# A planner's durations set anew: restarts, row groups, chained instructions and steps between engines

## The chip, the cores and the metric

The kernel runs on one core of one Trainium2 chip. The metric is the device time of one execution in microseconds (us), as a median over runs. One execution was also profiled, and all rows below come from that one.

## The reference, cut to what matters

A transformer layer works on x of 8 x 512 x 256 in f32. It is layer-normed; then an attention part and a feed-forward part are added to x.

```python
xn = _layernorm(x)
# attention, 16 heads of 16: three branches
k_c, v_c = blocks(k) @ Wck, blocks(v) @ Wcv        # 32 blocks of 16 tokens
out_c = softmax(mask(q @ k_c.T / 4)) @ v_c         # compressed
top_idx = top_k(logits_c, 4)                       # 4 blocks for each query
out_s = softmax(q @ k[top_idx].T / 4) @ v[top_idx] # selected
out_l = softmax(window(q @ k.T / 4, 32)) @ v       # local window
out = (g0 * out_c + g1 * out_s + g2 * out_l) @ Wo
# feed-forward: product-key experts and a gated layer
sc, ix = top_k(einsum(xn @ Wq, keys), 8)           # two halves, 4 heads
idx, scores = best 8 of the 8 x 8 sums             # of 1024 experts
w = silu(xn @ down_embed[idx]) * softmax(scores)
mlp = silu(xn @ Wg + bg) * (xn @ Wu + bu) @ Wd + bd
x = x + out + mlp + w @ up_embed[idx]
```

## The kernel before

The work is cut into 8 rows of 512 tokens (the batch), 32 tiles of 128 tokens (4 to a row) and 16 halves of 256 tokens. For each row, `layernorm`, `prepare_keys` and `prepare_values` make the transposed input xnT, keys, values and gates. For each tile, `queries` and `logits` compute the compressed logits and the maxima of the scores by block (bm) and by window (ml); `select` picks the four blocks and extends the queries (ext, qx) by the mask; `weights` makes score blocks of 128 x 128 for all 16 heads and takes their exponential into wT; `products` multiplies wT with the values; `compressed` and `finish` normalise (rzn), gate and turn the heads back to tokens through `by_token` (results atc and at). `choose_experts` finds the best keys with MAX8 and FIND_INDEX8 and turns them into tables; `route` spreads them over 1024 experts on VectorE (big) and GpSimd (gw); `experts` applies all 1024 experts densely (aT). For each half, `hidden` makes the gated layer (xg, hT) in eight slices, whose weights wb come by DMA one slice at a time, and multiplies with Wd; `project` multiplies aT with up_embed (ue_s) and the attention with Wo, and adds to yo.

Heads are 16 wide and lie in row groups of 32 partitions. The score and product matmuls therefore use only a quarter of the array, and four of them with different `tile_position` can run beside each other; the program marks such stretches with `con.share = 4`. In the trace an f32 matmul leaves two records, a transpose or a bf16 matmul one.

Each engine works through its own queue in the order in which the program wrote it[...]. The order is written by a planner, the class `Conductor`, while the program is built. Every stage above is a Python generator that goes over its items and is a job of its own. At a `yield` it names the engine that it needs next and the buffers or events that it needs first; what lies between two yields is a step, issued without interruption. `run` (line 237) asks `begin` (227) for each job's earliest start by the plan's clock. Of the jobs that can start no later than 0.12 us (`NEAR`, 172) after the first, the one with the lowest rank is taken (about the oldest tile), and `step` (220) lets it issue its instructions. Every instruction passes `book` (184), which adds an assumed duration to its engine's time `at` and so sets when engine, result and buffers are taken to be free. The assumptions are constants: a fixed part and a part by element for each engine (170, 171), a cost by column for matmuls, a divisor for row groups, an extra for a few slow operations, and `HOP` (169), the time from a result on one engine to its use on another. `book` also keeps VectorE's two-input instructions that read no PSUM and GpSimd's work apart, as the two are taken to share a port. A wrong duration breaks nothing, since semaphores hold whatever comes early: it makes an order in which an instruction stands in its queue ahead of what it waits for, and all behind it waits too.

PSUM is given out as two pairs of banks for scores and four single banks for all the rest (283, 284). After the set-up the planner's clocks are put to zero (436), then the jobs are added and run.

```python
    HOP = {"PE": 0.3, "DVE": 0.2, "ACT": 0.23, "POOL": 0.2, "SP": 2.5, None: 0.0}
    ...
            first = min(s for s, _ in ready)
            s, j = min((r for r in ready if r[0] <= first + self.NEAR), key=lambda r: r[1].rank)
```

Of the kernel before, what the change touches and what calls it, by code (L numbers as in the profile page):

```python
# [9 lines left out]
BF16 = mybir.dt.bfloat16  # L10
# [6 lines left out]
P = 128  # L17
# [89 lines left out]
class Event:  # L107


    def __init__(self):  # L110
        self.time = None
# [52 lines left out]
class Conductor:  # L164
# [1 line left out]

    HOP = {"PE": 0.3, "DVE": 0.2, "ACT": 0.23, "POOL": 0.2, "SP": 2.5, None: 0.0}
    FIXED = {"DVE": 0.07, "ACT": 0.07, "POOL": 0.26}  # L170
    EACH = {"DVE": 1.04e-3, "ACT": 0.83e-3, "POOL": 1.9e-3}
    NEAR = 0.12

    def __init__(self, psum):
        self.psum = psum
        self.at = dict.fromkeys(("PE", "DVE", "ACT", "POOL", "SP"), 0.0)
        self.busy = dict.fromkeys(self.at, 0.0)
        self.port = {"DVE": (0.0, 0.0), "POOL": (0.0, 0.0)}
        self.jobs, self.cur, self.share = [], Job(None, 0), 1

    def later(self):
        return self.cur.end + self.HOP[self.cur.eng]

    def book(self, eng, op, args, kw):
        aps = [a for a in [*args, *kw.values()] if hasattr(a, "shape")]
        n = max(int(np.prod(a.shape[1:])) for a in aps)
        if eng == "PE":
            if op == "transpose":
                cost = 0.11
            else:  # L190
                n = int(np.prod(args[2].shape[1:]))
                cost = (n * 0.42e-3 if args[2].dtype == BF16 else max(n, 32) * 1.68e-3) / self.share
        elif eng == "SP":
            cost = 0.06
        else:
            each = self.EACH[eng]
            if eng == "DVE" and all(a.dtype == BF16 for a in aps):
                each /= 2
            cost = self.FIXED[eng] + each * n
            if op in ("match_replace", "max_index", "tensor_tensor_reduce"):  # L200
                cost += 0.08
        j = self.cur
        start = max(self.at[eng], j.end + (self.HOP[j.eng] if eng != j.eng else 0.0))
        if eng == "POOL" or eng == "DVE" and op in ("tensor_tensor", "scalar_tensor_tensor") and not any(
                a.tensor is self.psum.tensor for a in aps):

            s, e = self.port["DVE" if eng == "POOL" else "POOL"]
            if s <= start:
                start = max(start, e)
            self.port[eng] = (start, start + cost)  # L210
        self.at[eng] = start + cost
        self.busy[eng] += cost
        j.end, j.eng = start + cost, eng
# [4 lines left out]
        self.step(j, None)  # L218

    def step(self, j, got):  # L220
        self.cur = j
        try:
            j.req = j.gen.send(got)
        except StopIteration:
            self.jobs.remove(j)

    def begin(self, j):
        eng, *res = j.req
        s = j.end + (self.HOP[j.eng] if eng is not None and eng != j.eng else 0.0)
        for r in set(res):  # L230
# [6 lines left out]
    def run(self):  # L237
        while self.jobs:
# [9 lines left out]
            else:  # L248
                j.end = max(j.end, s - self.HOP[j.eng])
            got = [r.take() for r in j.req[1:]]  # L250
# [1001 lines left out]
```

## Time and profile before

| what | value |
|---|---|
| median of 3 runs | 1812.65 us (1808.81 to 1814.56) |
| the profiled execution's own time | 1813.57 us |
| its span, first to last instruction | 1811.8 us |
| TensorE (PE) busy | 1622.0 us, 90% |
| VectorE (DVE) busy | 1478.4 us, 82% |
| GpSimd (POOL) busy | 1012.4 us, 56% |
| ScalarE (ACT) busy | 686.5 us, 38% |
| mean granted TensorE clock | 0.97 |
| DMA | 31 GB/s on average |
| chain of work that ended last | PE 55%, DVE 36%, ACT 3% |

PE is the matmul engine, and PEld its weight loads, which run beside it. Line numbers in the rows are all L160, since every instruction passes one helper; the tile names tell the groups apart. A row of the groups or of the timeline gives output<-input, shapes, count and duration; in brackets stands how long the engine was idle before and what released it. Durations of instructions that follow each other overlap in part on VectorE and TensorE, so the distance of two starts says more about what one occupies than its own duration. The first 60 us are set-up and loading.

### The profile page before, as it was taken

To read this page: it belongs to the slowest core of one execution; us is meant where nothing else is said; L and a number is where in the kernel's file an instruction comes from. 1 tells how busy PE (TensorE), PEld (TensorE's weight loads), DVE (VectorE), ACT (ScalarE), POOL (GpSimd) and SP (SyncE) were. 2 spreads that over 40 slices of the span, in tenths; PEclk is the share of its full clock that TensorE was granted. 3 is DMA by queue.
4 is the path that set the end of the run, shared out by engine and by line. 5 is a ranking of instruction groups with operands and counts; after the bars stand their busy time and mean duration, and the time that the engine had idled before them with its cause. 6 is when DMAs were issued, how large, how long until landed. Compare 5 with 4: busy or idle time off the path is not lost.

```text
span 1811.8 us, 47633 instructions
## 1 busy us (share of the span) xinstructions
PE 1622.0 (90%) x19208; PEld 1246.5 (69%) x19208; DVE 1478.4 (82%) x5292; ACT 686.5 (38%) x1370; POOL 1012.4 (56%) x789
## 2 busy tenths in 40 slices
PE   3889879899899998999989998989979999898969
PEld 2667757777677766767667676766757777676757
DVE  2598799886977889898898967788897897979892
ACT  1344323444335243352343533344324434433233
POOL 2066546646475365665476754656647456575644
PEclk9999989999999999999999998999989999998989
DMA  5001001111001100001011110101001010100001
GB/s 181 10 21 37 19 19 31 31 40 24 24 25 37 37 26 25 24 26 38 16 34 31 32 31 20 36 26 37 25 18 31 15 40 28 31 19 24 25 11 32
DMA packets 55069, 56.12 MB, mean 31 GB/s; under 512 B 21696, under 2 KB 38080, under 8 KB 54848
## 3 DMA queue, kind: packets, MB, share of 16 engines
q1 hardware_dynamic: 54848, 53.07, 9.8%
q8 instruction: 151, 2.47, 0.6%
q14 instruction: 70, 0.57, 0.1%
HBM read 48.02 MB, written 4.19 MB: 29 GB/s over the span
## 4 chain that ended last, share of the span: by engine, by line
PE 55%; DVE 36%; ACT 3%; issue 3%; POOL 1%; DMA 1%; SPq 0%; DVEq 0%; ACTq 0%; POOLq 0%
PE psum L160 55%; DVE bm L160 6%; DVE big L160 4%; DVE pick L160 3%; DVE ixu L160 2%; DVE ml L160 2%; DVE mr L160 2%; DVE aT L160 2%; ACT wT L160 2%; DVE junk L160 2%; DVE hT L160 1%; DVE sums L160 1%; DVE top L160 1%; DVE at_x L160 1%; DVE xg L160 1%
## 5 line engine op out<-in xcount | busy, mean ns | idle before, releaser
L160 POOL TENSOR_TENSOR big<-big,ed 128x1024 f32<-128x1024 f32 x224 | 486.1, 2170 | 411.9 <-DVE big L160 359.2
L160 ACT ACTIVATE wT<-psum 128x1024 f32<-128x1024 f32 x224 | 217.6, 1021 | 167.6 <-PE psum L160 167.6
L160 PE MATMUL psum<-xnT,wb 128*128 128x256 f32 x1024 | 255.2, 393 | 9.1 <-DVE hT L160 5.6
L160 POOL TENSOR_TENSOR gw<-gw,big 128x1024 f32<-128x1024 f32 x96 | 228.1, 2376 | 7.0
L160 DVE TENSOR_REDUCE bm<-psum 128x32 f32<-128x512 f32 (+2 forms) x224 | 199.1, 911 | 32.3 <-PE psum L160 32.1
L160 PEld LDWEIGHTS psum<-xnT,wb 128*128 128x128 f32 x1024 | 191.7, 196 | 46.7 <-DVE hT L160 8.2
L160 DVE SCALAR_TENSOR_TENSOR big<-rc 128x1024 f32<-128x1024 f32 x128 | 167.6, 1309 | 19.5 <-POOL gw L160 19.5
L160 PE MATMUL psum<-wT,v 128*32 128x128 f32 x3584 | 138.4, 279 | 25.7 <-ACT wT L160 24.9
L160 PE MATMUL psum<-qx,k 32*128 32x128 f32 (+1 forms) x4352 | 149.6, 271 | 11.0 <-DVE ml L160 9.1
L160 PEld LDWEIGHTS psum<-qx,k 32*128 32x128 f32 (+1 forms) x4352 | 123.8, 175 | 38.9 <-issue 17.8
L160 PEld LDWEIGHTS psum<-wT,v 128*32 128x32 f32 x3584 | 86.6, 109 | 78.7 <-ACT wT L160 50.6
L160 PE MATMUL psum<-xnT,deT_s 128*128 128x128 f32 x1024 | 131.9, 284 | 5.0 <-DVE aT L160 2.7
L160 PEld LDWEIGHTS psum<-xnT,deT_s 128*128 128x128 f32 x1024 | 126.0, 199 | 12.1 <-DVE aT L160 3.7
L160 PE MATMUL psum<-wd_s,hT 128*128 128x256 f32 x512 | 121.1, 382 | 0.0
L160 DVE SCALAR_TENSOR_TENSOR aT<-aT,psum 128x512 f32<-128x512 f32 x128 | 87.3, 682 | 38.9 <-ACT aT L160 31.4
L160 PE MATMUL psum<-k,q 32*128 32x384 f32 (+3 forms) x1024 | 113.9, 486 | 5.2 <-DVE ml L160 3.7
L160 PE MATMUL psum<-ue_s,aT 128*128 128x256 f32 x512 | 117.1, 381 | 0.0
L160 ACT ACTIVATE xg<-psum,bgh 128x256 f32<-128x256 f32 x128 | 60.7, 474 | 142.3 <-PE psum L160 140.1
L160 PEld LDWEIGHTS <-cbf 128*128 128x128 bf16 x856 | 69.1, 102 | 58.7 <-issue 30.6
L160 PEld LDWEIGHTS psum<-ue_s,aT 128*128 128x128 f32 x512 | 95.2, 190 | 15.5 <-issue 2.0
L160 PEld LDWEIGHTS psum<-wd_s,hT 128*128 128x128 f32 x512 | 94.1, 190 | 15.1 <-issue 2.6
L160 ACT COPY qx<-psum 128x512 f32<-128x512 f32 x80 | 47.0, 587 | 140.1 <-PE psum L160 126.9
(161 smaller groups left out, 3170.5 us busy)
## 6 DMA issues: line engine op xcount, KB each, us to landing
wb<-in_wgu SPq DMA_DIRECT2D x128, 256.0 KB, 2.6
xl<-in_x SPq DMA_DIRECT2D x8, 512.0 KB, 3.9
yo<-in_x SPq DMA_DIRECT2D x32, 128.0 KB, 2.1
out<-yo SPq DMA_DIRECT2D x32, 128.0 KB, 1.7
vl<-v SPq DMA_DIRECT2D x96, 8.5 KB, 1.8
deT_s<-in_deT SPq DMA_DIRECT2D x1, 1024.0 KB, 5.2
wd_s<-in_wd SPq DMA_DIRECT2D x1, 1024.0 KB, 7.6
ue_s<-in_ue SPq DMA_DIRECT2D x1, 1024.0 KB, 10.0
```

The costliest lines, as they stand in the source:

```text
L160: return f(*a, **k)
```

## The change

Only the planner's assumptions change; no instruction is added, removed or altered.

- `HOP` becomes shorter for PE (0.3 to 0.25), DVE (0.2 to 0.17), ACT (0.23 to 0.2) and POOL (0.2 to 0.15).
- `PART`: the first matmul or transpose of each step costs 0.1 more (a restart). `step` sets the mark `fresh`.
- Row groups: the shared time is no longer a plain quarter, but 1.22 quarters where the stationary operand has 128 columns, and 1.1 quarters otherwise. The costs by column go to 1.69e-3 (f32) and 0.43e-3 (bf16), a transpose to 0.112, and the lower limit of 32 columns becomes 64 divided by the share.
- `AFTER`: an instruction on DVE, ACT or POOL that reads the tensor which the instruction before it on that engine wrote costs 0.083, 0.1 or 0.05 more. `written` keeps that tensor.
- A reciprocal costs 0.08 more, and a ScalarE instruction with a tensor as scale or bias 0.09 more.
- GpSimd's cost by element goes from 1.9e-3 to 2.0e-3.

```diff
-    HOP = {"PE": 0.3, "DVE": 0.2, "ACT": 0.23, "POOL": 0.2, "SP": 2.5, None: 0.0}
+    HOP = {"PE": 0.25, "DVE": 0.17, "ACT": 0.2, "POOL": 0.15, "SP": 2.5, None: 0.0}
     FIXED = {"DVE": 0.07, "ACT": 0.07, "POOL": 0.26}
-    EACH = {"DVE": 1.04e-3, "ACT": 0.83e-3, "POOL": 1.9e-3}
+    EACH = {"DVE": 1.04e-3, "ACT": 0.83e-3, "POOL": 2.0e-3}
+
+    AFTER = {"DVE": 0.083, "ACT": 0.1, "POOL": 0.05}
+    PART = 0.1
     NEAR = 0.12
...
+        self.written, self.fresh = dict.fromkeys(self.at), True
...
             if op == "transpose":
-                cost = 0.11
+                cost = 0.112
             else:
                 n = int(np.prod(args[2].shape[1:]))
-                cost = (n * 0.42e-3 if args[2].dtype == BF16 else max(n, 32) * 1.68e-3) / self.share
+                cost = n * 0.43e-3 if args[2].dtype == BF16 else max(n, 64 // self.share) * 1.69e-3
+                if self.share > 1:
+
+                    cost *= (1.22 if args[1].shape[-1] == P else 1.1) / self.share
+            if self.fresh:
+                cost += self.PART
+            self.fresh = False
...
-            if op in ("match_replace", "max_index", "tensor_tensor_reduce"):
+            if op in ("match_replace", "max_index", "tensor_tensor_reduce", "reciprocal"):
                 cost += 0.08
+            if eng == "ACT" and any(hasattr(kw.get(k), "shape") for k in ("scale", "bias")):
+                cost += 0.09
+            to = kw["out"] if "out" in kw else args[0]
+            if any(a.tensor is self.written[eng] for a in aps if a is not to):
+                cost += self.AFTER[eng]
+            self.written[eng] = to.tensor
...
     def step(self, j, got):
-        self.cur = j
+        self.cur, self.fresh = j, True
```

## The prediction

> **What bounds the kernel now.** The diff alters only the numbers with which the program plans its order, so the instructions stay and only their order on each engine can move. I read the page's busy shares first, then the stretches, then TensorE's waits, then single steps.
>
> The busy shares of the page:
>
> ```profile
> PE 1622.0 (90%) x19208; PEld 1246.5 (69%) x19208; DVE 1478.4 (82%) x5292; ACT 686.5 (38%) x1370; POOL 1012.4 (56%) x789
> ```
>
> TensorE is nearly full; VectorE comes next. Stretches of the same trace (columns: length, then busy time of PE, PEld, DVE, ACT, POOL, then granted clock, DMA share, GB/s):
>
> ```profile
> 800.00:900.00 100.00, 96.17 (x1120) 72.04 (x1108) 83.76 (x318) 38.65 (x77) 57.71 (x46) 0.98 0.09 29
> 1300.00:1400.00 100.00, 87.46 (x1073) 65.25 (x1062) 86.08 (x262) 34.80 (x66) 59.45 (x45) 0.93 0.07 23
> 1400.00:1500.00 100.00, 97.06 (x1051) 75.26 (x1048) 87.45 (x331) 40.05 (x87) 52.29 (x41) 1.00 0.10 29
> 1600.00:1700.00 100.00, 86.83 (x859) 66.32 (x858) 87.58 (x281) 31.91 (x63) 60.48 (x45) 0.93 0.09 26
> ```
>
> The same work runs with TensorE 97% busy at clock 1.00 in one stretch and 87% at 0.93 in another. From 100 us to the end TensorE is busy for 1560.2 of 1712 us: 151.8 us idle, which another order can win or enlarge, and 0.03 x 1712 = 51 us of lost clock. What ended the waits (us, times, longest), in the same window:
>
> ```profile
> PE psum L160 <- DVE atc L160: 31.1, 10, 8.3
> PE psum L160 <- ACT wT L160: 24.9, 41, 3.6
> PE psum L160 <- DVE aT L160: 17.5, 14, 2.8
> PE psum L160 <- DVE at L160: 13.3, 13, 2.8
> PE psum L160 <- DVE ml L160: 12.8, 18, 1.8
> PE psum L160 <- DVE hT L160: 8.7, 8, 2.4
> ```
>
> These six rows make 108.3 of the 151.8 us. None is a DMA. They are many short waits for VectorE and ScalarE: the order put a TensorE step ahead of a result that came later than planned.
>
> **The change part by part: how wrong is the plan now?** Its own sums can be held against rows.
>
> *Four row groups and restarts.* One score block is 16 matmuls of 128 columns (32 records in the trace). The old plan counts 16 x 128 x 1.68e-3 / 4 = 0.86 us, the new one 16 x 128 x 1.69e-3 x 1.22 / 4 + 0.1 = 1.16. The timeline has (start, duration):
>
> ```profile
> 504.90 1.17 PE L160 MATMUL psum<-qx,k 32*128 32x128 f32 x32
> 506.17 1.94 ACT L160 ACTIVATE wT<-psum 128x1024 f32<-128x1024 f32 x2 [1.36 <-PE psum L160]
> 507.24 0.65 PE L160 MATMUL psum<-wT,v 128*32 128x128 f32 x16 [1.17 <-ACT wT L160]
> ```
>
> The new count fits. A product step of 8 goes from 0.43 to 0.58 (shown: 0.65, with the overlapping tail). Over the run: scores 1792 matmuls x 12.2 ns = 22 us, products 1792 x 5.7 = 10, window logits 163,840 columns x 0.095 ns = 16, other grouped matmuls 6, and 9 for 1.69, 0.43 and 0.112. PE steps per row of 512 tokens: 24 to prepare it, 29 for each of four tiles, 69 in logits, selection, scores and products; 209 x 8 rows x 0.1 = 167 us. The plan's TensorE total rises by about 230, from about 1340 (counts of the groups by the old formula) to 1570. The trace has 1594 after the first 60 us, of which 3% is lost clock, so about 1546 at full clock. Part of the 167 is too much: 16 records of ue_s took from 515.57 to 519.12 = 3.55 us, 8 x 0.433 plus one restart, while the plan charges four. Three in each of the two such loops of a tile, with the last step of the projection: 7 x 32 x 0.1 = 22 us that no trace row has.
>
> *Instructions that follow their own result.* Another piece of the timeline:
>
> ```profile
> 1748.94 0.41 DVE L160 TENSOR_REDUCE row<-pick 128x32 f32<-128x256 f32 x1
> 1749.39 0.19 DVE L160 TENSOR_REDUCE rz<-row 128x4 f32<-128x32 f32 x1
> 1749.61 0.18 DVE L160 RECIPROCAL rz<-rz 128x4 f32<-128x4 f32 x1
> 1749.82 0.23 DVE L160 TENSOR_TENSOR ed<-ed,rz 128x64 f32<-128x64 f32 x1
> ```
>
> Starts lie 0.45, 0.22 and 0.21 apart. Old plan: 0.34, 0.10, 0.07. New: 0.42, 0.19, 0.24. About 24 such instructions a tile in the expert choice, 4 in selection, 3 in the three normalisations, 4 in the hidden layer, 1.5 in the layer norm: 36.5 x 32 x 0.083 = 97 us, and 144 reciprocals x 0.08 = 12: VectorE's planned load grows by 109 us.
>
> *The rest.* The 256 ScalarE instructions with a bias by partition go from 0.28 to 0.37 (in the timeline the xg step starts at 504.00 and its follower at 504.37), 23 us on an engine that is 38% busy. GpSimd's 1024-element products go from 2.21 to 2.31, with 0.05 more after their own result; rows of 2170, 2376 and 1901 ns lie around both, so nothing is decided there, 56% busy. Steps between engines shrink by 0.03 to 0.05 us: TensorE's 0.1 is now in the step itself, so for a TensorE producer the sum grows. SyncE's figures stay; its loads move with the jobs that they serve. No wait of TensorE after 100 us is put down to a DMA, so I cost moved loads at nothing: two wb buffers ahead hide their 2.6 us; uncovered, one load would cost up to that.
>
> *What it is worth on the chip.* No instruction gets shorter; a gain is only wait removed. The bounds are an order as good as the best stretch, 97.06 against the mean 91.7 of 100 to 1700 us (1712 x (1 - 91.7/97.06) = 95 us gained), and one as poor as the worst, 84.06 in 200 to 300 (1712 x (91.7/84.06 - 1) = 156 us lost); neither is likely over a whole run. I take one quarter of the 108.3 us of waits, 27 us: the chain steps and blocks above, which the old plan counts 20 to 60% short, stand ahead of most of them, but queues and buffers stay, and a wait removed is partly found again at VectorE, which is 84% busy from 100 us on (1432.8 of 1712) and is late next. A quarter is near a second reading: the better half of the sixteen 100 us stretches averages 94.2, and an order that did that throughout would win 1712 x (1 - 91.7/94.2) = 45 us, of which I keep about 60%. Clock comes on top: 27 of 151.8 us idle is 18%, of 51 us lost clock that is 9; I count 4[...]. Sum -31. Against the profiled execution (span 1811.8, own time 1813.6) and the median 1812.65, which is 0.9 us lower, that is 1782.
>
> *A rule against the change.* The Trainium skill (Perfetto Trace Analysis, Optimization Strategy) says that a gap repeating on the engine that should be full can mean that there is too little PSUM for the next tile. The largest row above, 31.1 us, is of this kind: a step wants a bank that the step on atc releases. By the rule, counting durations adds no bank, and these 31 us stay. But at the longest of them the timeline shows what stood ahead on VectorE:
>
> ```profile
> 1107.79 1.22 DVE L160 TENSOR_REDUCE bm<-psum 128x64 f32<-128x1024 f32 x1
> ...
> 1113.61 0.48 DVE L160 SCALAR_TENSOR_TENSOR atc<-psum,gt,rzn 128x256 f32<-128x256 f32 x1
> ...
> 1114.15 1.86 PE L160 MATMUL psum<-big,cbf 128*128 128x256 bf16 x8 [8.30 <-DVE atc L160]
> ```
>
> From 1105.9 to 1114.1 VectorE works without a pause on other jobs, and the instruction that frees the bank comes last. That is order, so part of the row can go. By the rule the quarter would be of 77 us (19), and the time 1790.
>
> **The rivals.**
> *No real change* (0.08). All planned durations grow together, TensorE 17%, VectorE some 9%, and the order keeps its quality: 1807 to 1818, say 1811. For it: the limits (four single banks, two pairs, 0.12 us of choice between jobs) are untouched. Against it: ratios between engines shift, and 1672 TensorE steps are ordered anew; an exact tie is unlikely.
> *A large gain* (0.11). The plan now knows that TensorE bounds it, always has several ready steps, and takes the oldest tile. TensorE at 95.5% and clock 0.99: 1712 x (1 - 91.7/95.5) = 68, and some 7 of clock: 1738.
> *Slower* (0.34). The new plan sees about 1570 on TensorE against some 1310 on VectorE (the old formulas over the rows' sizes, 1200, plus 109) and believes that VectorE has slack. It doesn't count all of it: the trace has 1433 us there after 100 us, and a row like the 128x1024 SCALAR_TENSOR_TENSOR, mean 1309 ns against a free 1136, shows the waiting beside GpSimd that stays uncounted. With shorter steps between engines (0.17 after VectorE instead of 0.2) the order then puts more TensorE steps directly behind late VectorE results. The place: expert choice and the bank behind atc. The price: a wait like the two of 8.3 and 8.2 us in the trace, plus lost clock: the granted clock was 0.74 and 0.83 in the 20 us around them, so 5.2 and 3.4 us lost, 12 to 13 each. Three more cancel the 31 us won elsewhere; five more, from there, make 1839. The decision: whether waits over 4 us number more than five instead of two.
>
> **How the numbers follow.** Moderate gain 0.47 (1750 to 1806), large gain 0.11, no change 0.08, slower 0.34 (1819 to 1870). 0.3% is 5.4 us, about what a measurement of this kernel can tell from no change. So faster 0.58, same 0.08, slower 0.34; time 1782, in the likeliest case's own range 1750 to 1806. The range 1738 to 1842 leaves out half of the large gains and a third of the losses, 0.06 and 0.12.
>
> **What would show it.** Right: TensorE's busy time from 100 us on stays near 1560, its idle time there falls from 152 to about 125, the rows for wT, at, aT and hT shrink together, granted clock is at or above 0.97, and VectorE's idle share falls. Wrong: the row for atc grows or waits over 4 us multiply (the slower rival); the same rows with the same sums (no change); or TensorE's waits shrink while its busy time grows, so that restarts were moved and not saved. The steps I trust least are the quarter and the belief that a plan with truer durations orders better at all; the sums of the new durations I trust.

## The result, and the profile after

The changed kernel takes 1824.27 us (median of 7 runs, 1818.63 to 1828.14) against 1812.66 before (7 runs): ratio 1.0057, with an interval of 1.0040 to 1.0073. It is slower by 11.6 us; I had forecast 31 us faster. The measured time lies inside the range that I gave, on the side of the rival.

The busy shares of the changed kernel's page:

```profile
PE 1625.9 (89%) x19208; PEld 1251.9 (69%) x19208; DVE 1477.1 (81%) x5292; ACT 685.1 (38%) x1370; POOL 1009.3 (55%) x789
```

The same work is done in the same busy time. One stretch holds all of the change, from 100 us to the end (columns: length, busy PE, PEld, DVE, ACT, POOL, clock, DMA share, GB/s):

```profile
100.00:1826.00 1726.00, 1561.73 (x18667) 1205.67 (x18665) 1436.90 (x5124) 661.22 (x1313) 991.50 (x756) 0.97 0.09 28
```

TensorE is idle for 1726 - 1561.7 = 164.3 us there, before 151.8: 12.5 us more waiting, at the same granted clock. What ended the waits in that window (us, times, longest):

```profile
PE psum L160 <- DVE aT L160: 24.4, 16, 4.8
PE psum L160 <- DVE atc L160: 22.0, 16, 6.2
PE psum L160 <- DVE at L160: 17.4, 14, 3.3
PE psum L160 <- DVE hT L160: 16.1, 12, 2.5
PE psum L160 <- ACT wT L160: 15.3, 39, 1.2
PE psum L160 <- DVE xn L160: 12.4, 7, 2.5
PE psum L160 <- DVE ml L160: 9.6, 16, 2.0
PE psum L160 <- ACT k L160: 7.5, 9, 1.0
```

Three of the six rows on which I had built fell (atc by 9.1, wT by 9.6, ml by 3.2), three rose (aT by 6.9, at by 4.1, hT by 7.4): together 104.8 instead of 108.3. The rest went from 43.5 to 59.5. A row for xn, which wasn't there, and more for k and vc belong to the start of a new row of tokens; acs and q, which every tile has, grew too. So the order is another one, with other waits, and not one with less waiting.

The longest wait of the new order is a single one of 6.2 us for atc. The next four are one step that repeats: in the stretches around 687, 1125 and 1561 us the same TensorE step waits 4.79 us, and around 254 us 3.89. The timeline around 687 us:

```profile
686.32 2.34 POOL L160 TENSOR_TENSOR big<-big,ed 128x1024 f32<-128x1024 f32 x1 [4.14 <-DVE big L160]
...
686.49 2.55 DVE L160 TENSOR_TENSOR gt<-pg,bga_s 128x4 f32<-128x4 f32 x3
...
689.65 1.83 DVE L160 TENSOR_TENSOR gt<-gt,gm 128x12 f32<-128x12 f32 x1
...
691.41 0.67 DVE L160 SCALAR_TENSOR_TENSOR aT<-aT,psum 128x512 f32<-128x512 f32 x1
...
692.14 2.07 PE L160 MATMUL psum<-xnT,deT_s 128*128 128x128 f32 x8 [4.79 <-DVE aT L160]
```

The small gate instructions work on 4 and 12 numbers in each partition. The group of the first, over the whole run (shortest, median and longest in ns), shows what they take:

```profile
L160 DVE TENSOR_TENSOR gt<-pg,bga_s x24: 148/154/2206, 91.0 to 1562.7; 128x4 f32<-128x4 f32 x24
```

154 ns is usual; here VectorE starts one 0.17 us after GpSimd has begun a product of 2.3 us, and ends when GpSimd is through. Then it happens again behind the next one. Behind them stands aT, and behind aT stands TensorE. `book` knows the shared port, but by the plan's own clock the small instructions start a little earlier than the product, so no wait is planned.

### The profile page after: what moved, and what is told of

The parts are those of the page before. It is cut to its first block, busy times and chain, and to the rows that moved or that the text cites. A ratio compares the mean times of both kernels' runs of the same rounds, so it can differ in the third digit from the quotient of the medians.

```text
span 1826.3 us, 47731 instructions
## 1 busy us (share of the span) xinstructions
PE 1625.9 (89%) x19208; PEld 1251.9 (69%) x19208; DVE 1477.1 (81%) x5292; ACT 685.1 (38%) x1370; POOL 1009.3 (55%) x789
## 4 chain that ended last, share of the span: by engine, by line
DVE 46%; PE 43%; issue 5%; ACT 4%; POOL 2%; SPq 1%; DMA 1%; DVEq 0%; POOLq 0%; ACTq 0%
PE psum L160 43%; DVE bm L160 8%; DVE big L160 5%; DVE mr L160 3%; DVE ixu L160 3%; DVE pick L160 3%; DVE aT L160 2%; DVE junk L160 2%; DVE ml L160 2%; DVE at_x L160 2%; ACT wT L160 2%; DVE top L160 1%; DVE sums L160 1%; DVE hT L160 1%; DVE gt L160 1%
## 5 line engine op out<-in xcount | busy, mean ns | idle before, releaser
L160 POOL TENSOR_TENSOR gw<-gw,big 128x1024 f32<-128x1024 f32 x96 | 232.3, 2420 | 7.1
L160 DVE SCALAR_TENSOR_TENSOR big<-rc 128x1024 f32<-128x1024 f32 x128 | 174.6, 1364 | 8.6 <-POOL gw L160 8.6
L160 PE MATMUL psum<-qx,k 32*128 32x128 f32 (+1 forms) x4352 | 155.3, 272 | 7.2 <-DVE ml L160 5.7
L160 PE MATMUL psum<-xnT,deT_s 128*128 128x128 f32 x1024 | 137.7, 292 | 22.4 <-DVE aT L160 21.0
L160 PEld LDWEIGHTS psum<-qx,k 32*128 32x128 f32 (+1 forms) x4352 | 127.7, 176 | 36.4 <-issue 19.0
L160 PEld LDWEIGHTS psum<-xnT,deT_s 128*128 128x128 f32 x1024 | 129.7, 205 | 28.8 <-DVE aT L160 24.0
L160 PE MATMUL psum<-wT,v 128*32 128x128 f32 x3584 | 133.2, 278 | 15.3 <-ACT wT L160 14.2
L160 DVE SCALAR_TENSOR_TENSOR xg<-psum,xg 128x256 f32<-128x256 f32 x128 | 53.4, 417 | 80.9 <-ACT psum L160 79.3
L160 PE MATMUL psum<-k,q 32*128 32x384 f32 (+3 forms) x1024 | 104.8, 470 | 4.6 <-DVE ml L160 3.9
```

The costliest lines, as they stand in the source:

```text
L160: return f(*a, **k)
```

## The experiments

Three theories were held against each other: *new draw* (the change only draws another order out of the same greedy planner, good or bad by chance); *a bad part* (shorter steps between engines, or restarts counted too often); *the port* (the one collision above). Later came *buffers* and *truer is better*. To say beforehand what new draw expects, I laid the changed plan's own durations over each kernel's order and added them up ("reckoned"); by that measure the order of before is 1751 us long and the changed one 1743, not counting the set-up. All ratios are to the kernel before on the same chip.

**Parts alone.** The first takes only the steps between engines:

```diff
-    HOP = {"PE": 0.3, "DVE": 0.2, "ACT": 0.23, "POOL": 0.2, "SP": 2.5, None: 0.0}
+    HOP = {"PE": 0.25, "DVE": 0.17, "ACT": 0.2, "POOL": 0.15, "SP": 2.5, None: 0.0}
```

> The kernel before with the four shorter steps between engines (0.25, 0.17, 0.2, 0.15) and nothing else of the change. Theory 'new draw' (the change only draws another order from the same planner; no part of it is bad in itself): within about 1% of before on either side; the order, reckoned with the changed plan's own durations, is 5 us longer than the order of before, so some 1817. Theory 'short steps' (steps between engines that are too short put TensorE's instructions ahead of results that come late): at least 1822, and the whole loss of 11.6 us is found here.

Measured: 0.9963 (0.9948 to 0.9978), faster than before. Shorter steps alone don't cost time; new draw had the sign wrong, with 5 us more reckoned and 7 fewer measured.

The second has TensorE's part only (against the changed kernel):

```diff
-    HOP = {"PE": 0.25, "DVE": 0.17, "ACT": 0.2, "POOL": 0.15, "SP": 2.5, None: 0.0}
+    HOP = {"PE": 0.3, "DVE": 0.2, "ACT": 0.23, "POOL": 0.2, "SP": 2.5, None: 0.0}
-    EACH = {"DVE": 1.04e-3, "ACT": 0.83e-3, "POOL": 2.0e-3}
+    EACH = {"DVE": 1.04e-3, "ACT": 0.83e-3, "POOL": 1.9e-3}
-    AFTER = {"DVE": 0.083, "ACT": 0.1, "POOL": 0.05}
+    AFTER = {"DVE": 0.0, "ACT": 0.0, "POOL": 0.0}
...
-            if op in ("match_replace", "max_index", "tensor_tensor_reduce", "reciprocal"):
+            if op in ("match_replace", "max_index", "tensor_tensor_reduce"):
...
-                cost += 0.09
+                cost += 0.0
```

> Only TensorE's durations of the change (restart 0.1, row groups by 1.22 and 1.1, columns, transposes); steps between engines and all else as before. 'New draw': reckoned with the changed plan's durations this order is 32 us longer than that of before, so 1845; the parts don't add up to the whole. 'Restarts overcounted' (charging each step 0.1 although steps that run on have none misleads the order): slower than before by 10 to 15 us, the loss of the whole change, since the other parts are harmless. 'Short steps': at or below 1813.

Measured: 1.0167 (1.0152 to 1.0182), 30 us more: the 32 that were reckoned, and three times the loss of the whole change. Its stretch from 100 us on, in the columns of before, has 1746.6 - 1570.1 = 176.5 us of idle TensorE:

```profile
100.00:1846.60 1746.60, 1570.11 (x18679) 1214.86 (x18677) 1411.55 (x5124) 663.63 (x1313) 1005.46 (x756) 0.97 0.09 27
```

The third has the other engines' part (TensorE's new costs by column stay in it):

```diff
-    HOP = {"PE": 0.25, "DVE": 0.17, "ACT": 0.2, "POOL": 0.15, "SP": 2.5, None: 0.0}
+    HOP = {"PE": 0.3, "DVE": 0.2, "ACT": 0.23, "POOL": 0.2, "SP": 2.5, None: 0.0}
...
-    PART = 0.1
+    PART = 0.0
...
-                    cost *= (1.22 if args[1].shape[-1] == P else 1.1) / self.share
+                    cost *= 1.0 / self.share
```

> Only the durations of the other engines (own result, reciprocal, bias by partition, GpSimd's element) with TensorE's columns at 1.69e-3 and 0.43e-3, but no restart and no factor for row groups, and the steps between engines as before. 'New draw': reckoned with the changed plan's durations 28 us longer than before, so 1841. 'Restarts overcounted' and 'short steps': 1813 or better, as VectorE's chain is counted truly.

Measured: 1.0067 (1.0050 to 1.0084), a loss as reckoned in sign, at less than half the size. The three parts add to -7 + 30 + 12 = 35 us where the whole costs 10; they don't add up (the costs by column, which the second and the third share, were not run alone), so no part is seen to have an effect of its own that it carries along.

**The same durations, other choices.** `NEAR` decides between jobs that can start almost at once and has nothing to do with durations.

```diff
-    NEAR = 0.12
+    NEAR = 0.04
```

> The kernel before with all its old durations; only the choice between jobs is narrower (0.04 us after the first that can start, instead of 0.12). No duration is truer than before. 'New draw': reckoned with the changed plan's durations this order is 48 us shorter than that of before, so about 1765: a setting that has nothing to do with durations moves the time by several times what the change did. 'Restarts overcounted' and 'short steps' say nothing of it and leave it within 5 us of 1813.

> The changed kernel, all new durations, with the choice between jobs narrowed to 0.04 us. 'New draw': reckoned with its own durations 12 us shorter than the changed kernel; ratio to before about 1.000, and slower than the kernel before with the same choice (0.981). Theory 'truer is better, the choice was set for the old durations': at or below the 0.981 of the old durations with 0.04.

With 0.05 in place of 0.04:

> The kernel before with the choice at 0.05 instead of 0.04 (which gave 0.981) or 0.12. 'New draw': reckoned with the changed durations 6 us longer than before, 54 us longer than with 0.04: ratio about 1.003, so that one hundredth of a microsecond moves the time by 2%. Rival 'a narrow choice is better in itself': near 0.981 again.

> The changed kernel with the choice at 0.05. 'New draw': reckoned with its own durations 20 us shorter than the changed kernel, ratio about 0.995. 'Truer is better': below 0.985.

| durations | 0.12 | 0.04 | 0.05 |
|---|---|---|---|
| old | 1 | 0.9807 (0.9795 to 0.9820) | 1.0051 (1.0031 to 1.0071) |
| new | 1.0057 (1.0040 to 1.0073) | 0.9935 (0.9913 to 0.9957) | 0.9903 (0.9884 to 0.9921) |

One hundredth of a microsecond in the choice moves the old plan by 2.4%, four times the change. The means by row are 0.995 and 0.997. *Truer is better* gets no support from these three pairs (it wins one), and *a narrow choice is better in itself* is wrong for the old durations, while both narrower choices were faster for the new ones. New draw had expected 0.974 (1765 us) and 1.003 for the old durations and 1.000 and 0.995 for the new; it had the direction right where it expected one, and is off by up to 0.7%, as much as the change itself. The kernel before with 0.04, 1781.10 us, beats both kernels. Its stretch from 100 us to its end:

```profile
100.00:1786.00 1686.00, 1542.42 (x18649) 1195.45 (x18648) 1488.16 (x5115) 661.29 (x1309) 1003.36 (x756) 0.98 0.10 28
```

TensorE idles 143.6 us there, 8 fewer than before, its busy time is 18 shorter at a clock of 0.98, and VectorE is busy for 88% instead of 84%. So most of its gain in this stretch, 18 of 26 us, isn't waiting but shorter busy time of the same instructions. Other orders differ in this too. Over all sixteen traces, from 100 us to the end, TensorE idles between 142.6 us (old at 0.04 with more buffers, below) and 176.5 (TensorE alone), and is busy between 1541.1 (other engines alone) and 1570.1 (TensorE alone). The mean granted clock of these executions (0.962 to 0.983) goes only in part with the busy time: new at 0.05 has 1550.3 us at 0.971, the changed kernel 1561.7 at the same clock. Why is not shown.

**The collision alone.** The changed kernel's order was written out, job by job, and kept. In seven rows of tokens one step moved. As a sketch of VectorE's queue, not of the program's text:

```diff
-    DVE: vc, gt gt gt, gm gm, gt, aT
+    DVE: vc, aT, gt gt gt, gm gm, gt
```

> The changed kernel with its order written out and kept, but in seven places VectorE's small gate instructions (gt, gm) stand behind the next instruction on aT instead of ahead of it; TensorE's, ScalarE's and GpSimd's orders are untouched. Theory 'port' (in four rows these 128x4 instructions start just behind a 2.3 us GpSimd product, last up to 2.2 us instead of 0.15, and hold up the instruction on aT for which TensorE waits 3.9, 4.8, 4.8 and 4.8 us): 16 to 19 us less than the changed kernel, so about 1806 on a chip where before is 1813, ratio 0.996; the loss of the change is this one collision. Rival 'given back' (what waits there waits elsewhere): ratio stays at 1.005 to 1.006.

Measured: 1.0001 (0.9987 to 1.0014); the loss against before is gone. The stretch from 100 us on and two of TensorE's waits there:

```profile
100.00:1807.30 1707.30, 1548.87 (x18647) 1197.83 (x18647) 1426.82 (x5111) 659.22 (x1309) 992.11 (x756) 0.98 0.10 28
...
PE psum L160 <- ACT qx L160: 11.2, 4, 3.0
PE psum L160 <- DVE aT L160: 6.0, 11, 0.8
```

aT fell from 24.4 to 6.0, the 18.4 us that the port theory had named. But 11.0 came back in four waits at the next step (three of 3.0 us and one of 2.2), for qx, which had 0.2 us in the changed kernel. The timeline shows why:

```profile
683.46 1.83 DVE L160 TENSOR_TENSOR gt<-gt,gm 128x12 f32<-128x12 f32 x1
...
685.32 0.21 ACT L160 ACTIVATE gt<-gt 128x12 f32<-128x12 f32 x1 [10.10 <-DVE gt L160]
685.44 0.57 ACT L160 COPY qx<-psum 128x512 f32<-128x512 f32 x1
...
686.06 0.45 PE L160 MATMUL psum<-qx,k 32*32 32x32 f32 x32 [3.00 <-ACT qx L160]
```

The small instructions still take long behind GpSimd, 1.97 us for the first three and 1.83 for the last. Now ScalarE's exponential of the gates waits for them, and behind it in ScalarE's queue stands the copy of qx that TensorE needs. So both theories held in part: over half of the wait is given back, and yet the time of before is reached.

Waiting is only a part of what was won. TensorE idles 158.4 us (1707.3 - 1548.9), 6 fewer than in the changed kernel; its busy time is 12.9 us shorter, at a clock of 0.979 against 0.971, and the clock would account for that in this pair (estimate: 1561.7 x 0.971 / 0.979 = 1549). These two profiled executions lie 19 us apart, the medians 10. The clock was 0.973 to 0.979 in the 14 runs of this order and 0.970 to 0.975 in the 7 of the changed kernel; why it is higher is open. That the moved step takes back the loss is measured; that it does so by its waits alone is not, and an equally small move elsewhere, to compare with, was not run.

**Restarts only where they are.** Here a step that runs on from the same job's step isn't charged:

```diff
-            if self.fresh:
+            if self.fresh and not (self.last is self.cur and self.at["PE"] >= self.cur.end):
                 cost += self.PART
-            self.fresh = False
+            self.fresh, self.last = False, self.cur
```

> The changed kernel, but the 0.1 us of a restart is charged only where a TensorE step doesn't run on directly from the step before of the same job; the 22 us that no trace row has are gone from the plan. 'Restarts overcounted': the loss of the change goes, ratio 1.000 or below. 'New draw': a truer duration is again only another order; reckoned with the changed durations it is 11 us longer than the changed kernel, so about 1.012.

Measured: 1.0006 (0.9995 to 1.0017). That agrees better with overcounted restarts than with what was reckoned. But its waits show another order, not the changed one with something removed: aT and at have shrunk, and atc is longer than in either kernel (22.0 in the changed one, 31.1 before). In all TensorE idles 148.5 us there (1809.6 - 100 - 1561.1), 16 fewer than in the changed kernel, at a clock of 0.963 instead of 0.971.

```profile
PE psum L160 <- DVE atc L160: 38.8, 10, 7.4
PE psum L160 <- DVE ml L160: 13.8, 14, 2.3
PE psum L160 <- ACT wT L160: 13.3, 31, 1.2
PE psum L160 <- DVE aT L160: 10.1, 10, 1.7
```

Two more pairs, at 0.04 and 0.05, went the other way:

> As the run with the restart charged only where it is, but with the choice at 0.04; its partner is the changed kernel at 0.04 (ratio 0.9935). 'Restarts overcounted': the truer restart wins some 0.5% here too, ratio about 0.988. 'New draw': reckoned with the changed durations 27 us longer than its partner, so slower than it: 1.003 to 1.009.

> The same with the choice at 0.05; its partner is the changed kernel at 0.05 (ratio 0.990). 'Restarts overcounted': about 0.985. 'New draw': reckoned 4 us longer than its partner, 0.990 to 0.995.

Measured: 1.0098 (1.0076 to 1.0119) where its partner has 0.9935, and 1.0005 (0.9992 to 1.0018) where its partner has 0.9903. The truer count won half a per cent once and lost 1.6 and 1.0% in the other two. At 0.05 both theories missed: 1.0005 is above what either expected. A truer count of restarts gives no better order as such, so the overcount is not shown to be the cause.

**The port for all, and more buffers.**

```diff
-        if eng == "POOL" or eng == "DVE" and op in ("tensor_tensor", "scalar_tensor_tensor") and not any(
+        if eng == "POOL" or eng == "DVE" and op in (
+                "tensor_tensor", "scalar_tensor_tensor", "tensor_scalar", "tensor_copy") and not any(
```

> The changed kernel, and VectorE's one-input instructions that read no PSUM (xn, the cast ix, mr) are also planned not to run beside GpSimd, as the trace has them (xn 0.40 us free, up to 2.06 beside GpSimd). 'Truer is better': below 0.995, as the waits for xn (12.4 us) go. 'New draw': reckoned with the changed durations 4 us longer than the changed kernel, with the port counted as well 13 us shorter; ratio 0.998 to 1.008.

Measured: 0.9984 (0.9971 to 0.9996). Better than the changed kernel, but not by what truer is better asked for; it lies where new draw had it. TensorE's waits for xn are gone, as asked; others took their place (15.3 for wT and 9.6 for ml in the changed kernel):

```profile
PE psum L160 <- ACT wT L160: 35.0, 44, 3.4
PE psum L160 <- DVE ml L160: 27.8, 32, 2.5
```

The changed kernel with two buffers lg:

```diff
-    lgs = stock("lg", 1, [P, H, 4 + NB])
+    lgs = stock("lg", 2, [P, H, 4 + NB])
```

> The changed kernel with two buffers lg instead of one. Theory 'buffers' (TensorE's waits come from too few places, not from durations): the plan loses 22 us of TensorE's planned waiting, ratio about 0.994. Rival: the plan uses the second buffer and meets other waits, ratio 1.005 to 1.006.

Measured: 0.9981 (0.9968 to 0.9994), between the two theories. With the best order so far and a third aT beside it:

> The kernel before with the choice at 0.04 (0.981), two buffers lg and three aT. 'Buffers': below 0.975. 'New draw': reckoned with the changed durations 6 us longer than with 0.04 alone; ratio 0.982 to 0.985.

Measured: 0.9831 (0.9805 to 0.9858), against 0.9807 without them: beside that order these buffers gain nothing.

**How far the reckoning carries.** For the fourteen changed orders, reckoned against measured difference to before, in us (the ratio's distance from 1, times 1813; old and new are the durations, the number is the choice; the order written out isn't among them):

| order | reckoned | measured |
|---|---|---|
| changed | -7 | +10 |
| steps between engines alone | +5 | -7 |
| TensorE alone | +32 | +30 |
| other engines alone | +28 | +12 |
| old at 0.04 / new at 0.04 | -48 / -19 | -35 / -12 |
| old at 0.05 / new at 0.05 | +6 / -27 | +9 / -18 |
| restart where it is, 0.12 / 0.04 / 0.05 | +4 / +8 / -23 | +1 / +18 / +1 |
| port for all / two lg / old at 0.04 with buffers | -4 / -29 / -42 | -3 / -3 / -31 |

The correlation with the kernel before as a fifteenth point is 0.87. The changed durations, which made no better order, tell good orders from bad ones fairly well, to 11 us on average and 26 at worst.

## Why the prediction was wrong

- **The sums of the durations were right, and they didn't matter.** By its own clock the old plan ends at 1560 us, the new one at 1743; on the chip the parts after 60 us take 1752 and 1766. The plan's error shrank from 192 to 23 us, as the rows had promised. What I took from it was wrong.
- **The step that failed is the quarter of the 108.3 us.** I took wrong durations to be the cause of the waits, so that true ones would remove 27 us of them. The six rows lost 3.5 us and the others gained 16: 12.5 us more waiting, and with it the 4 us of clock didn't come (0.97 before and after). The plan itself didn't hold the gain: by the new durations the old order is 1751 us long and the new one 1743, so only 7 to 8 of the 27 us were even planned. In the new plan TensorE idles for 167 us, and nothing in the planner looks for a better order: of the jobs that can start first it takes the oldest. The three pairs of choices show the rest: orders drawn with the old durations lie between 0.981 and 1.005, with the new ones between 0.990 and 1.006.
- **"A gain is only wait removed" was too narrow.** It held for the change (busy 1560.2 and 1561.7 us). But where an order did gain 26 us from 100 us on, old at 0.04, 18 of them were shorter busy time.
- **The slower rival had the right place on the chip, but the wrong one in the program, and the wrong mark.** It blamed VectorE's uncounted waiting beside GpSimd and late VectorE results ahead of TensorE. That is what happened; but at the gates and aT, not at the expert choice, and the row for atc, named as the sign, fell from 31.1 to 22.0. Waits over 4 us went from two to four (6.2 and three of 4.8), not over five. And it blamed shorter steps between engines, which alone gave 0.9963. Two of its numbers were loose: five waits of 12 to 13 us more than the 1782 make some 1844, not 1839, and the row with a mean of 1309 ns has a median of 1217 in the same trace, so the waiting in it is smaller than the 1136 made it look.
- **"No real change" I gave 0.08.** I held a tie for unlikely, and it was not one; but the order's quality stayed about the same, as that rival said, and a draw of that quality can fall on either side.
- **The rule on PSUM.** It was read as speaking for a wait that stays. The wait for atc shrank with no bank added, so order does move it, yet the time didn't follow. On buffers in SBUF, two lg gave 0.9981 instead of 1.0057 once, and nothing beside the order at 0.04. More PSUM wasn't tried, as all eight banks are given out.
- **Over-charged restarts**, which I had put at 22 us, are not shown to be the cause: taking them out helped one order of three.

Open remains whether many draws would show a small mean gain from truer durations: three pairs with a spread of 2.4% can't tell 0.5%. Open is also why the reckoning misses single orders by 20 us and more (for the changed kernel it missed by 17, and moving one step took back 10), and why the same instructions are busy for longer in one order than in another.

## What to carry to other kernels

A greedy planner's order is much like a draw. Judge a new cost by several orders (here: neighbouring choices), not by one, before you believe that it helped or hurt. True durations are of use as a yardstick for orders made in many ways: here the order with the lowest reckoning, 48 us below before, was also the fastest. Lay the new durations over the old order first; that says, before any run, what the new plan itself expects to win. After each new order look for long waits that repeat once in a period: one step in the wrong place of a queue, moved by hand in seven places, was worth the whole difference here.

## What the runs showed of the hardware

A VectorE instruction on 4 numbers in each partition lasts 148 to 154 ns, and up to 2206 when it starts just behind a GpSimd product. The same holds for one-input instructions that read only SBUF (shortest, median and longest in ns, changed kernel):

```profile
L160 DVE TENSOR_SCALAR xn<-xl,mv,rs x32: 393/410/2058, 27.7 to 1411.5; 128x256 f32<-128x256 f32 x32
...
L160 DVE CAST ix<-ixu x32: 297/300/1927, 78.8 to 1743.1; 128x64 bf16<-128x64 uint32 x32
```

The Trainium skill (SBUF — State Buffer, SBUF: two separate sides) describes an exclusive lock for a whole instruction, held by whichever starts first, GpSimd or a VectorE instruction that has two SBUF inputs or runs in a 2-port mode. The rows of two inputs agree with it; that the one-input ones run in such a mode is not shown here, but they too last as long as GpSimd's product when they start behind one (the xn at 971.89 us starts 0.43 us behind a product of 2.34 and takes 2.06). So the planner's rule, which counted two-input instructions only, was too narrow. I hadn't expected that a wait of 2 us could hang on which of two engines starts 0.17 us earlier.
